# Reordering the side work of a fused RNN, SSM, LSTM and adapter kernel

## The chip, the cores and the metric

The kernel runs on one core of a Trainium2 chip, as one launch. The metric is the device time in microseconds. The engines named below are PE (TensorE: matmuls, with PEld for its weight loads), DVE (VectorE), ACT (ScalarE), POOL (GpSimd) and SP, which here only issues DMAs. Every engine works through its own instruction list in the order in which the kernel wrote it; semaphores make an instruction wait for another engine.

## The reference, cut to what matters

Four layers with residuals, over x of shape (4, 1024, 512), batch B = 4, T = 1024, D = 512. The first and the third are recurrences over the 1024 steps.

```python
x = x + rnn(x)        # h = tanh(x_t @ Wx + b + h @ Wh), h0 = cond
x = x + ssm(x)        # below
x = x + lstm(x)       # A = x_t @ Wx + b + h @ Wh; i, f, o, g; c; h = o * tanh(c)
x = x + adapt(x)      # out = x @ (base + x_a x_b^T), one layer matrix per batch row
...
# ssm: a convolution over 4 steps, two projections, and a state of 64 channels
proj = conv @ Wp + bp;  B_t = softplus(proj[..., :N]);  C_t = tanh(proj[..., N:])
u = x @ Ws + bs
state = decay * state + dt * b_t * u_t;  y_t = c_t * state
out = y @ Wo + bo
# adapt: x_a and x_b come from the condition alone
h = gelu(layernorm(cond) @ w1 + b1);  xw = h @ w2 + b2     # w2: 512 x 8192
```

## The kernel before, in words

All four layers run at once, on different parts of the sequence. Time is cut into 32 chunks of TC = 32 steps. `do_pass(c)` runs the 32 LSTM steps of chunk c; in the same steps the RNN runs LEAD = TC + 20 = 52 steps ahead, and between the two the kernel puts what the chunks between need: projections, the SSM of chunk c + 1, the inputs of the LSTM, and the adapter of chunk c - 1. In the first 52 steps (pass -2 from step 12 on, and pass -1) there is no LSTM; only the RNN and preparation run. I call these the lead.

The order is written out by hand (`manual_schedule`), so the lists in the code are the order on each engine. In one step of `do_pass` they are:

- PE: the LSTM's 96 matmuls (`lstm_mm`, L362; bf16, the state as three bf16 parts), then the jobs placed as "pe", then `rnn_mm` (L337), then whatever the step's "early" jobs issue.
- DVE: for half A of the LSTM state the transpose (L379), sum (L384), products, cell, h (L408) and two splits (L191), then the same for half B. Jobs placed as "gap" come between B's cell and B's h. After B come `rnn_pre` (transpose L345, add L346), then the jobs placed as "end", then "early" jobs.
- ACT: the tanh of gates and cell, two small copies for the next step, the RNN's tanh (L349), and the ACT parts of the jobs.

A job is a triple of step, place and function. Those of a regular pass, before:

- `adapt_jobs`: four adds at the end of steps 1, 2, 5 and 6; the four products `ada` (L702, each 4 matmuls with 512 columns) in steps 16, 21, 22, 23; in the end place of 23 an ACT copy and four output DMAs.
- `ssm_jobs`: three adds x + h in steps 9 to 11; `taps` in 12 to 15 (16 matmuls with 128 columns each) and `skip` (8 matmuls) in 16; the softplus in 15 to 23; four scans, then y = state * dt * c, in place in tile w; then the output product in 24.
- `project0`: the RNN's input projection of chunk c + 3, 16 matmuls with 128 columns in each of steps 17 to 20.
- `input_jobs`: the LSTM's input product for 8 steps at a time, 4 matmuls with 512 columns a step (L318), in steps 0 to 11 and 25 to 28, followed by two transposes (L322) and two bias adds (L330).

fp32 matmuls show as two records each in the profile, bf16 ones as one.

The lead also prepares: the LSTM weights are loaded and split in three bf16 parts (`split_wh2`, ACT L276 and L280, DVE L277 and L281), one piece a step from step 5 to 20. `adapt_hidden` computes the hidden layer at step 30. From step 32 on `adapt_w2(j)` multiplies one piece of w2 (two ranks, 512 KB, four buffers) at a time: 16 matmuls with 64 columns, a copy on ACT, and the load of piece j + 4. Twelve pieces come in the lead, one every step and a half, and twenty in steps 0 to 19 of pass 0. `adapt_gather` brings the results into another layout by DMAs on POOL, `base_identity` adds 2 to a diagonal by 16 small DVE instructions, `adapt_sum` adds the gathered parts, and `adapt_layer` makes the layers, one of 16 tiles a step from step 25 of pass 0.

Of the kernel before, what the change touches and what calls it, by code (L numbers as in the profile page):

```python
# [14 lines left out]
P = 128  # L15
B, T, D = 4, 1024, 512
KC = D // P
# [3 lines left out]
TG = 8  # L21
LEAD = TC + 20
CT = 32
# [15 lines left out]
def cond_resid_kernel(ctx: ExitStack, tc: tile.TileContext, a: dict, out: bass.AP):  # L39
# [293 lines left out]
    def rnn_mm(c, t):  # L333
        h = h0[c % 2] if t else h0[(c - 1) % 2]
        for k in range(KC):
            for j in range(4):
# [4 lines left out]
                )  # L341

    def rnn_pre(c, t):
        tt, pre = tt0[0], pre0[t % 2]
        nc.vector.transpose(tt.rearrange("p c b -> p (c b)"), acc0)  # L345
        nc.vector.tensor_add(pre, xw0[c % 2][:, :, t, :], tt[:, :, :B])  # L346
# [71 lines left out]
    def ssm_jobs(c):  # L418
# [6 lines left out]
        def add(ms, t0, t1):  # L425
            t = lambda y: y[:, ms, t0:t1].rearrange("p c t b -> p c (t b)")
            v.tensor_add(t(x1[:, :, 3:, :]), t(x), t(h))  # L427


        jobs = [  # L430
            (9, "end", lambda: add(slice(0, 2), 0, TC - 4)),
            (10, "gap", lambda: add(slice(2, 4), 0, TC - 4)),
            (11, "end", lambda: add(slice(0, 4), TC - 4, TC)),
        ]
# [17 lines left out]
        cg, z, e, u, w, p = (sm(n) for n in ("cg", "z", "e", "u", "w", "p"))  # L452
        bt, vv, y = z, e, w
        v3, y3 = (t.rearrange("p (t b) -> p t b", b=B) for t in (vv, y))
        y_last = y3[:, TC - 1, :]
        jobs += [(12 + k, "pe", lambda k=k: taps(k)) for k in range(KC)]
        jobs.append((16, "pe", skip))

        def turn(n):
            cols = slice(n * TOK // 4, (n + 1) * TOK // 4)  # L460
            v.reciprocal(u[:, cols], u[:, cols])


        jobs += [
            (15, "end", lambda: act.activation(z, pb[:NS, 0, :], AF.Identity, bias=vec[:NS, 0:1])),
            (15, "end", lambda: act.activation(e, pb[:NS, 0, :], AF.Abs, bias=vec[:NS, 0:1])),
            (16, "end", lambda: act.activation(e, e, AF.Exp, scale=-1.0)),
            (16, "end", lambda: act.activation(u, e, AF.Copy, bias=2.0)),
            (18, "end", lambda: act.activation(cg, pb[NS:, 0, :], AF.Tanh, bias=vec[NS:, 0:1])),
            (18, "end", lambda: v.tensor_mul(u, u, e)),  # L470
            (18, "end", lambda: v.tensor_mul(w, u, u)),
            (18, "end", lambda: act.activation(p, w, AF.Copy, scale=2.0 * SERIES[-1])),
            (23, "end", lambda: act.copy(s1, y_last)),
        ]
# [7 lines left out]
        for b in range(B):  # L482
# [4 lines left out]
        chain += [  # L487
            lambda: v.scalar_tensor_tensor(y, y, dt, cg, ALU.mult, ALU.mult),
        ]
        place = lambda n: ("gap", "end", "end")[n % 3]  # L490
        jobs += [(17 + n // 3, place(n), lambda n=n: turn(n)) for n in range(4)]
        jobs += [(19 + n // 3, place(n), f) for n, f in enumerate(chain)]

# [27 lines left out]

    xr = w1.rearrange("p k (a r n) -> p (k a) r n", a=2, n=P // 2).rearrange(
        "p (h d) r n -> p h d r n", h=2
    )
    raw = [work.tile([P, D], F32, name=f"raw{i}", tag=x) for i, x in enumerate(("x3", "x4"))]
# [52 lines left out]
    def adapt_w2(j):  # L578


        half, hd, rg = j // (KC * RANK // WR), j // (RANK // WR) % KC, j % (RANK // WR)
        ps = bank("pp", [P, P // 2])
        for k in range(KC):
            for t in range(4):
                n0 = P // 2 * (t % 2)
                nc.tensor.matmul(
                    ps[CT * t : CT * (t + 1), :], hid[:, k, :], w2[j][:, t // 2, k, n0 : n0 + P // 2],
                    start=(k == 0), stop=(k == KC - 1),
                )
        nc.scalar.copy(xr[:, half, hd, rg], ps)  # L590
        if j + W2_BUFS < NW2:
            load_w2(j + W2_BUFS)

    def adapt_gather(half):

        for t in range(4):
            for g in range(RANK // WR):
                nc.gpsimd.dma_start(
                    out=raw[half].rearrange("(b r) n -> b r n", r=32)[:, WR * g + t // 2].rearrange(
                        "b (d h n) -> b h d n", d=KC, h=2  # L600
                    )[:, t % 2],
                    in_=xr[CT * t : CT * t + B, half, :, g],
                )
# [59 lines left out]
    at_step(21, load_base)  # L663
    at_step(20, fold_conv)
    for half in range(2):
        at_step(27 + half, lambda half=half: adapt_bias(half))
    at_step(24, adapt_center)
    at_step(25, adapt_norm)
    at_step(26, lambda: nc.scalar.activation(b2[:, 3], b2[:, 3], AF.Copy, scale=2.0))
    for k in range(KC):  # L670
        at_step(26 + k, lambda k=k: double_g(k))
    at_step(30, adapt_hidden)
    NPRE = 12
    for j in range(NW2):
        f = lambda j=j: adapt_w2(j)
        if j < NPRE:
            at_step(32 + 3 * j // 2, f)
        else:
            at(0, j - NPRE, f)
        if j % (NW2 // 2) == NW2 // 2 - 1:  # L680
            at(0, j - NPRE, lambda half=j // (NW2 // 2): adapt_gather(half))
    for half in range(2):
        at(0, 24, lambda half=half: adapt_sum(half))
    at(0, 23, base_identity)
    for n in range(B * KC):
        c, t = divmod(25 + n, TC)
        at(c, t, lambda n=n: adapt_layer(n % B, n // B))


    def adapt_jobs(c, dst):  # L690
# [21 lines left out]

        jobs = [((1, 2, 5, 6)[m], "end", lambda m=m: add(m)) for m in range(KC)]
        jobs += [((16, 21, 22, 23)[k], "pe", lambda k=k: mm(k)) for k in range(KC)]
        return jobs + [(23, "end", end)]


    def input_jobs(c, n, t):
        ps = {}

        def mm(k):
            if not ps:

                ps[0] = bank("proj2", [P, D], tag=("ada", "po")[n % 2], bufs=1)
            input_mm(c, n, k, ps[0])

        last = t + KC - 1
        return [(t + k, "pe", lambda k=k: mm(k)) for k in range(KC)] + [
            (last, "end", lambda: input_turn(c, n, 0, ps[0])),
            (last + 1, "gap", lambda: input_turn(c, n, 2, ps[0])),  # L730
            (last + 1, "end", lambda: input_bias(c, n, 0)),
            (last + 2, "gap", lambda: input_bias(c, n, 2)),
        ]


    def do_pass(c, first=0, src=None, dst=None):
# [5 lines left out]
        if -1 <= c < NCHUNK - 1:  # L742
            jobs += ssm_jobs(c + 1)
            jobs += input_jobs(c + 1, 0, 25)
        if src is not None:
            jobs.append((12, "end", lambda: load_x(c + 4, src)))
        if c + 3 < NCHUNK:
            for m in range(KC):
                mm, end = project0(c + 3, m)
                jobs += [(17 + m, "pe", mm), (17 + m, "end", end)]  # L750
        if lstm:
            for n in range(1, TC // TG):
                jobs += input_jobs(c, n, KC * (n - 1))

# [5 lines left out]
        for t in range(first, TC):  # L760
# [10 lines left out]
            if rnn:  # L771
                rnn_mm(*r)
            if lstm:
                A.transpose()
# [105 lines left out]
```

## Time and profile before

| | us |
|---|---|
| median of 3 runs | 4822.73 (4818.03 to 4823.34) |
| the profiled execution | 4822.13 |
| its span | 4820.3 |
| TensorE busy | 4609.6 |
| DVE busy | 3864.6 |
| ACT busy | 1494.4 |
| LSTM matmuls L362, 98304 records | 2881.0 |
| RNN matmuls L337, 32768 records | 1109.8 |
| input products L318, 4096 records | 528.9 |

Busy time is what an engine's records cover; a matmul's record includes time in which the next one has already begun, so the distance from the start of one group to the start of the next says more. "Idle before, releaser" in a line names what ended an engine's wait. A releaser "issue" means that nothing the profile shows held the engine back. The table by stage has, for each stretch, its length, the busy time of PE, PEld, DVE, ACT and POOL with the number of instructions, the granted TensorE clock (1.00 is full), the share of the DMA engines and GB/s.

The instructions of TensorE are themselves fetched by DMA:

```profile
q8 instruction: 1149, 18.83, 1.6%
```

### The profile page before, as it was taken

The page shows a single profiled execution, that of the slowest core. Times are in us where ns is not written, and L with a number is a line of the kernel's source. Part 1 is how long each engine was busy: PE and PEld are TensorE (multiplying, and loading weights), DVE is VectorE, ACT ScalarE, POOL GpSimd, SP SyncE. Part 2 cuts the span into 40 slices and gives each one's busy share as a digit, 9 for nine tenths or more (in the row PEclk, how much of TensorE's full clock was granted, in tenths as well). Part 3 has the DMA queues.
Part 4 walks back from the last instruction along what each step waited for, and adds up shares of the span by engine and source line. Part 5 has one row for each costly group of instructions (what it writes and reads, how often), then busy time and mean ns, then how long its engine had stood idle before and what let it go on. Part 6 is the DMA issues. An engine that isn't in the chain of part 4 may idle for free.

```text
span 4820.3 us, 320719 instructions
## 1 busy us (share of the span) xinstructions
PE 4609.6 (96%) x147040; PEld 3536.0 (73%) x147040; DVE 3864.6 (80%) x18001; ACT 1494.4 (31%) x7661; POOL 53.5 (1%) x96
## 2 busy tenths in 40 slices
PE   6899999999999999999999999999999999999976
PEld 4777777777777777777777777777777777777754
DVE  3578888888888888888888888888888888888876
ACT  2223333333333333333333333333333333333322
POOL 2000000000000000000000000000000000000000
PEclk7999999999999999999999999999999999999999
DMA  6300000000000000000000000000000000000000
GB/s 146 115 9 9 9 7 9 7 9 9 9 7 9 7 9 9 9 7 9 6 9 9 9 7 9 7 9 9 9 7 9 7 9 9 9 4 6 6 6 7
DMA packets 38780, 67.41 MB, mean 14 GB/s; under 512 B 9056, under 2 KB 26080, under 8 KB 36400
## 3 DMA queue, kind: packets, MB, share of 16 engines
q1 hardware_dynamic: 34064, 46.68, 3.7%
q8 instruction: 1149, 18.83, 1.6%
q14 instruction: 207, 1.70, 0.1%
q0 software_dynamic: 2208, 0.19, 0.1%
q10 hardware_dynamic: 1152, 0.01, 0.0%
HBM read 38.34 MB, written 8.39 MB: 10 GB/s over the span
## 4 chain that ended last, share of the span: by engine, by line
PE 89%; DVE 8%; issue 1%; ACT 1%; DMA 0%; ACTq 0%; SPq 0%; DVEq 0%
PE acc L362 57%; PE acc L337 16%; PE proj L318 9%; PE pb L292 3%; PE proj L292 2%; DVE tt L379 2%; PE ada L702 2%; DVE gc L384 1%; DVE h L191 1%; DVE h L408 1%; DVE prod L395 1%; DVE gc L400 1%; DVE tt L345 0%; ACT x L709 0%; PE pl L624 0%
## 5 line engine op out<-in xcount | busy, mean ns | idle before, releaser
L362 PE MATMUL acc<-wh,h 128*12 128x256 bf16 x98304 | 2881.0, 273 | 145.8 <-DVE h L191 135.6
L362 PEld LDWEIGHTS <-h 128*12 128x12 bf16 x98304 | 2276.8, 88 | 702.6 <-DVE h L191 382.5
L379 DVE STREAM_TRANSPOSE tt<-acc 128x256 f32<-128x256 f32 x2048 | 918.8, 449 | 453.0 <-PE acc L362 334.9
L337 PEld LDWEIGHTS acc<-wh,h 128*4 128x4 f32 x32768 | 816.9, 87 | 505.1 <-issue 206.6
L337 PE MATMUL acc<-wh,h 128*4 128x128 f32 x32768 | 1109.8, 275 | 34.9 <-ACT h L349 25.2
L391 ACT ACTIVATE gc<-gc 128x32 f32<-128x32 f32 x2048 | 469.8, 229 | 1319.0 <-DVE gc L384 1233.0
L384 DVE TENSOR_REDUCE gc<-tt 128x32 f32<-128x128 f32 x2048 | 774.2, 378 | 35.3
L191 DVE TENSOR_TENSOR h<-h 128x8 f32<-128x8 f32 (+1 forms) x4098 | 681.2, 166 | 104.8
L405 ACT ACTIVATE th<-gc 128x8 f32<-128x8 f32 x2048 | 427.8, 209 | 826.2 <-DVE gc L400 826.2
L349 ACT ACTIVATE h<-pre 128x16 f32<-128x16 f32 x1024 | 221.3, 216 | 1149.7 <-DVE pre L346 1149.7
L318 PE MATMUL proj<-wx,x 128*32 128x512 f32 x4096 | 528.9, 592 | 0.6 <-DVE x L500 0.6
L408 DVE SCALAR_TENSOR_TENSOR h<-gc,th 128x8 f32<-128x8 f32 x2048 | 342.4, 167 | 141.3 <-ACT th L405 126.3
L345 DVE STREAM_TRANSPOSE tt<-acc 128x128 f32<-128x128 f32 x1024 | 316.2, 309 | 68.3 <-PE acc L337 65.2
L400 DVE SCALAR_TENSOR_TENSOR gc<-prod 128x8 f32<-128x8 f32 x2048 | 341.9, 167 | 35.5
L368 ACT COPY tt<-xw 128x32 f32<-128x32 f32 x2048 | 327.7, 207 | 0.0
L395 DVE SCALAR_TENSOR_TENSOR prod<-gc 128x16 f32<-128x16 f32 x2048 | 318.1, 155 | 0.0
L346 DVE TENSOR_TENSOR pre<-xw,tt 128x16 f32<-128x16 f32 x1024 | 179.8, 176 | 37.0
L292 PE MATMUL proj<-xin,wx 128*32 128x128 f32 x4096 | 144.9, 277 | 14.1 <-DMA wh<-in_Wh_dram 10.8
L292 PE MATMUL pb<-x,wp 128*32 128x128 f32 x4096 | 136.8, 273 | 3.3 <-DVE x L427 1.8
L702 PE MATMUL ada<-layer,x 128*32 128x512 f32 x1024 | 135.0, 600 | 3.0 <-DVE x L695 3.0
L292 PEld LDWEIGHTS proj<-xin,wx 128*32 128x32 f32 x4096 | 119.8, 112 | 16.5 <-DMA wh<-in_Wh_dram 10.7
L318 PEld LDWEIGHTS proj<-wx,x 128*32 128x32 f32 x4096 | 118.0, 110 | 6.2 <-DVE x L500 0.7
(116 smaller groups left out, 1152.7 us busy)
## 6 DMA issues: line engine op xcount, KB each, us to landing
layer<-in_w2T_dram SPq DMA_DIRECT2D x32, 512.0 KB, 3.5
xin<-in_xT_dram SPq DMA_DIRECT2D x128, 64.0 KB, 2.3
out_dram<-x SPq DMA_DIRECT2D x128, 64.0 KB, 1.7
layer<-in_Wh_dram SPq DMA_DIRECT2D x16, 256.0 KB, 10.0
wx<-in_Wx_dram SPq DMA_DIRECT2D x4, 1024.0 KB, 15.5
wx<-in_Wx_dram SPq DMA_DIRECT2D x4, 256.0 KB, 4.4
wh<-in_Wh_dram SPq DMA_DIRECT2D x4, 256.0 KB, 6.8
layer<-in_w_dram SPq DMA_DIRECT2D x4, 256.0 KB, 23.0
```

What stands on the lines that cost most here:

```text
L191: nc.vector.tensor_tensor(h[:, :, n], h[:, :, n - 1], upper(h[:, :, n - 1]), ALU.subtract)
L292: nc.tensor.matmul(dst[CT * j : CT * (j + 1)], columns(j), x, start=first, stop=final)
L318: nc.tensor.matmul(ps[CT * j : CT * (j + 1), :], tok, w[:, j], start=(k == 0), stop=(k == KC - 1))
L337: nc.tensor.matmul(acc0[CT * j : CT * j + B, :], h[:, k, (t - 1) % TC, :], wh0[:, k, j * P : (j + 1) * P], start=(k == 0), stop=(k == KC - 1),
L362: nc.tensor.matmul(acc2[mh][CT * j : CT * j + NP * B, :], parts, w[:, :, n0 : n0 + 2 * CT], start=(k == 0 and n == 0), stop=(k == KC - 1 a ...
L379: nc.vector.transpose(self.tt[:, :, :, B:].rearrange("p g c b -> p (g c) b"), acc2[self.m])
L384: nc.vector.tensor_reduce(self.gc[:, :4].rearrange("p g c b -> p (g c) b"), self.tt[:, :, :, : (1 + NP) * B].rearrange("p g c (s b) -> p ( ...
L391: nc.scalar.activation(self.gc[:, :4], self.gc[:, :4], AF.Tanh, scale=0.5)
L395: nc.vector.scalar_tensor_tensor(self.prod, self.gc[:, 0:2], 1.0, self.gc[:, 3:5], ALU.add, ALU.mult)
L400: nc.vector.scalar_tensor_tensor(self.c, self.prod[:, 1], 0.5, self.prod[:, 0], ALU.mult, ALU.add)
L405: nc.scalar.activation(self.th, self.c, AF.Tanh, scale=0.5)
L408: nc.vector.scalar_tensor_tensor(self.out[:, :, 0], self.gc[:, 2], 1.0, self.th, ALU.add, ALU.mult)
```

## The change

LEAD becomes TC + 24, so the RNN runs 56 steps ahead and the lead has 56 steps. In a regular pass the jobs move:

| | before | after |
|---|---|---|
| SSM adds | 9 end, 10 gap, 11 end | 5, 6, 7 end |
| `taps` | 12, 13, 14, 15 | 8, 10, 12, 14 |
| `skip` | 16 | 16 |
| `ada` products | 16, 21, 22, 23 | 17, 19, 21, 23 |
| `project0` | 17, 18, 19, 20 | 18, 20, 22, 30 |
| LSTM inputs 1, 2, 3 | 0-3, 4-7, 8-11 | 0-3, 4-7, 9, 11, 13, 15 |
| adapt adds | 1, 2, 5, 6 end | 0, 1, 2 end, 6 gap |
| copy of the last state | 23 end | 24 end |
| x load | 12 | 9 |

The scans write a tile of their own, `states`, and y goes to tile p. `adapt_w2` takes two pieces of w2 at once, with 128 columns a matmul, every third step from step 35 of the lead and every second step of pass 0; the gathers are half as many. `keep_busy` adds four matmuls with 512 columns, whose result nobody reads, behind `rnn_mm` in the first 32 steps. `adapt_layer` runs three times in four steps, from step 24. In the lead, steps of single preparations move by one.

```diff
-LEAD = TC + 20
+LEAD = TC + 24
...
+    idle = bank("idle", [P, D], tag="ada", bufs=1)
+    def keep_busy():
+        x = xin[0].rearrange("p c t b -> p (c t b)")
+        tiled(idle, lambda j: x[:, :CT], x)
...
-            (9, "end", lambda: add(slice(0, 2), 0, TC - 4)),
-            (10, "gap", lambda: add(slice(2, 4), 0, TC - 4)),
-            (11, "end", lambda: add(slice(0, 4), TC - 4, TC)),
+            (5, "end", lambda: add(slice(0, 2), 0, TC - 4)),
+            (6, "end", lambda: add(slice(2, 4), 0, TC - 4)),
+            (7, "end", lambda: add(slice(0, 4), TC - 4, TC)),
...
-        bt, vv, y = z, e, w
-        v3, y3 = (t.rearrange("p (t b) -> p t b", b=B) for t in (vv, y))
+        bt, vv, states, y = z, e, w, p
+        v3, y3 = (t.rearrange("p (t b) -> p t b", b=B) for t in (vv, states))
...
-        jobs += [(12 + k, "pe", lambda k=k: taps(k)) for k in range(KC)]
+        jobs += [(8 + 2 * k, "pe", lambda k=k: taps(k)) for k in range(KC)]
...
-            (23, "end", lambda: act.copy(s1, y_last)),
+            (24, "end", lambda: act.copy(s1, y_last)),
...
-            lambda: v.scalar_tensor_tensor(y, y, dt, cg, ALU.mult, ALU.mult),
+            lambda: v.scalar_tensor_tensor(y, states, dt, cg, ALU.mult, ALU.mult),
...
-        jobs += [(17 + n // 3, place(n), lambda n=n: turn(n)) for n in range(4)]
-        jobs += [(19 + n // 3, place(n), f) for n, f in enumerate(chain)]
+        jobs += [((16, "end"), (16, "end"), (17, "gap"), (17, "end"))[n] + (lambda n=n: turn(n),) for n in range(4)]
+        jobs += [(19 + (n + 1) // 3, place(n + 1), f) for n, f in enumerate(chain)]
...
-        ps = bank("pp", [P, P // 2])
+        ps = bank("pp", [P, P])
         for k in range(KC):
             for t in range(4):
-                n0 = P // 2 * (t % 2)
                 nc.tensor.matmul(
-                    ps[CT * t : CT * (t + 1), :], hid[:, k, :], w2[j][:, t // 2, k, n0 : n0 + P // 2],
+                    ps[CT * t : CT * (t + 1), :], hid[:, k, :], w2[j + t // WR][:, t % WR, k],
...
-        if j + W2_BUFS < NW2:
-            load_w2(j + W2_BUFS)
+        for n in range(j + W2_BUFS, min(j + W2_BUFS + 2, NW2)):
+            load_w2(n)
...
-    for j in range(NW2):
+    for j in range(0, NW2, 2):
         f = lambda j=j: adapt_w2(j)
         if j < NPRE:
-            at_step(32 + 3 * j // 2, f)
+            at_step(35 + 3 * j // 2, f)
         else:
-            at(0, j - NPRE, f)
+            at(0, j - NPRE + 1, f)
...
+    at(0, 21, base_identity)
     for half in range(2):
-        at(0, 24, lambda half=half: adapt_sum(half))
-    at(0, 23, base_identity)
+        at(0, 22 + half, lambda half=half: adapt_sum(half))
     for n in range(B * KC):
-        c, t = divmod(25 + n, TC)
+        c, t = divmod(24 + 4 * n // 3, TC)
...
-        jobs = [((1, 2, 5, 6)[m], "end", lambda m=m: add(m)) for m in range(KC)]
-        jobs += [((16, 21, 22, 23)[k], "pe", lambda k=k: mm(k)) for k in range(KC)]
+        jobs = [((0, 1, 2, 6)[m], ("end", "gap")[m // 3], lambda m=m: add(m)) for m in range(KC)]
+        jobs += [(17 + 2 * k, "pe", lambda k=k: mm(k)) for k in range(KC)]
...
                 mm, end = project0(c + 3, m)
-                jobs += [(17 + m, "pe", mm), (17 + m, "end", end)]
+                t = (18, 20, 22, 30)[m]
+                jobs += [(t, "pe", mm), (t, "end", end)]
...
-                jobs += input_jobs(c, n, KC * (n - 1))
+            jobs += input_jobs(c, 1, range(4), ((3, "end"), (4, "gap"), (4, "end"), (5, "gap")))
+            jobs += input_jobs(c, 2, range(4, 8), ((8, "gap"), (8, "end"), (9, "gap"), (9, "end")))
+            jobs += input_jobs(c, 3, range(9, 17, 2), ((15, "end"), (16, "gap"), (18, "gap"), (19, "gap")))
...
             if rnn:
                 rnn_mm(*r)
+            if c * TC + t < 8 - TC:
+                keep_busy()
```

## The prediction

> **What bounds the kernel now.** I read the totals and the chain of waits first, then the table by stage, then the timeline of single steps.
>
> ```profile
> PE 4609.6 (96%) x147040; PEld 3536.0 (73%) x147040; DVE 3864.6 (80%) x18001; ACT 1494.4 (31%) x7661; POOL 53.5 (1%) x96
> PE 89%; DVE 8%; issue 1%; ACT 1%; DMA 0%; ACTq 0%; SPq 0%; DVEq 0%
> ```
>
> That looks like a TensorE bound. One step of the middle says otherwise:
>
> ```profile
> 1503.64 0.45 DVE L379 STREAM_TRANSPOSE tt<-acc 128x256 f32<-128x256 f32 x1 [0.22 <-PE acc L362]
> 1504.40 1.03 PE L318 MATMUL proj<-wx,x 128*32 128x512 f32 x8
> 1505.26 1.05 PE L337 MATMUL acc<-wh,h 128*4 128x128 f32 x32
> 1506.22 2.80 PE L362 MATMUL acc<-wh,h 128*12 128x256 bf16 x96
> 1508.09 0.45 DVE L379 STREAM_TRANSPOSE tt<-acc 128x256 f32<-128x256 f32 x1 [0.23 <-PE acc L362]
> ```
>
> From transpose to transpose a step takes 4.45 us: a loop of LSTM matmuls, transpose, sum, tanh, products, h, splits and matmuls again. The last steps, which have no other TensorE work, take 4.45 us too, so the loop's latency is the bound. Side work fits in the gaps: 0.86 us of L318 and 0.86 of L337 (start to start) leave TensorE some 0.1 us. DVE has about 0.3 us in the "gap" place and 0.6 at the "end". A step is longer only where a job overflows its gap; those overflows are what a reordering can win.
>
> ```profile
> 0.00:162.15 162.15, 108.60 (x2774) 80.83 (x2777) 62.43 (x214) 44.08 (x131) 35.44 (x64) 0.82 0.58 142
> 162.15:331.31 169.16, 157.93 (x5193) 129.72 (x5184) 126.40 (x580) 47.21 (x256) 18.02 (x32) 0.99 0.18 56
> 331.31:485.50 154.19, 151.35 (x4586) 112.37 (x4578) 124.27 (x568) 45.84 (x237) 0.00 (x0) 1.00 0.03 8
> 485.50:4525.00 4039.50, 3962.84 (x127540) 3048.81 (x127535) 3341.01 (x15652) 1280.57 (x6631) 0.00 (x0) 1.00 0.03 8
> ```
>
> These stages are the lone RNN, pass 0, pass 1 and passes 2 to 29 (then 283 us for the last two passes, 12 for the tail). A pass without overflow is 32 x 4.453 = 142.5 us. Passes 2 to 29 take 4039.5 / 28 = 144.27, so 1.77 each is to be had; pass 0 is 26.7 over, pass 1 11.7.
>
> **The steady passes.** By step number, averaged over passes 3 to 28, the 1.77 lies in four places.
>
> ```profile
> 2432.76 1.03 PE L702 MATMUL ada<-layer,x 128*32 128x512 f32 x8
> 2433.61 0.93 PE L292 MATMUL pb<-x,ws 128*32 128x128 f32 x14
> 2468.09 0.59 ACT L709 COPY x<-ada 128x512 f32<-128x512 f32 x1
> 2468.58 0.19 ACT L473 COPY s<-w 64x4 f32<-64x4 f32 x1
> 2468.80 0.34 DVE L488 SCALAR_TENSOR_TENSOR w<-w,sp,cg 64x128 f32<-64x128 f32 x1 [0.90 <-ACT s L473]
> 1706.28 0.83 PE L362 MATMUL acc<-wh,h 128*12 128x256 bf16 x23 [0.29 <-issue]
> ```
>
> - Step 16, +0.76: one `ada` product and the `skip` matmuls share a step, 0.86 + 0.55 where 0.96 fits. After, `skip` keeps step 16 and `ada` goes to 17, 19, 21, 23, alone in each: 0.
> - Step 23, +0.48: y overwrites the states, so DVE waits 0.90 us for the copy of the last state, which stands behind the 0.59 us output copy on ACT; A's transpose is queued behind it. After, y has its own tile and the copy goes to step 24: 0. Late next is DVE's own work, a scan and y, which ends at 4.45: nothing to wait for.
> - Step 11, +0.09: the last add waits for the same step's RNN h and a 0.44 us turn follows. After, the add is at step 7 with no turn behind it, ending 4.46 into the step: 0 to 0.03.
> - Steps 13 to 20, +0.41 in all, irregular, idle put down to "issue". Instruction queue q8 moved 18.83 MB in 1149 packets: 64 bytes for each of TensorE's 294,080 records, 256 a packet. A step with 64 small records beside the 256 of LSTM and RNN uses 320, one with L318 or `ada` 272. The four tap steps and four projection steps follow each other, and the stalls start only at the second. Steps 0 to 11, at 272, have none. After, 320 and 272 alternate: 296 on average, between the two. Bounds: 0 (as at 272) and 0.41 (as now). The first tap step after the light ones costs 0.01, so I take 0.12.
>
> The moved DVE jobs make step 16 (0.44 in the gap, two reciprocals at the end), 18 and 19 (0.42 and 0.56) the fullest. Today's step 17 has 0.34 and 0.62 and costs nothing by itself. I count them zero, with 0.02 each above. Adapt adds and turns move one at a time to places with as much room; x loads on SP go three steps earlier, past nothing that waits. New pass: 142.65. Gain 28 x (144.27 - 142.65) = **45.4 us**. The last two passes have almost no overflow.
>
> **Pass 0.**
>
> ```profile
> 173.36 1.06 PE L337 MATMUL acc<-wh,h 128*4 128x128 f32 x32
> 174.24 0.63 PE L586 MATMUL pp<-layer,hid 128*32 128x64 f32 x32
> 174.68 2.58 PE L362 MATMUL acc<-wh,h 128*12 128x256 bf16 x87
> 339.41 1.12 PE L624 MATMUL pl<-xt,xt 8*128 8x512 f32 x2
> ```
>
> A w2 piece takes 0.44 us from start to start (32 records of 64 columns) and lengthens a full step by 0.35. A pair has 32 records of 128 columns. Here a rule speaks for more: the Trainium skill (TensorE: Matmul & The Clock Gate, "Wait — 56ns, not 53.3ns?") says that start-to-start never drops below about 25 ns, however small the matmul. By it 64 columns cost as much as 128 and pairs would halve the time. The row shows 14 ns for 64 columns and L337's 27 for 128, so a pair is 0.87 us, two pieces' worth. I take the row; by the rule it would be 3 to 6 us better. Ten pairs fall in steps 1, 3, ... 19; 17 and 19 have no product in pass 0. So 8 x 0.77 = 6.2 us against 20 x 0.35 = 7.
>
> The larger part is stalls: what these steps have beyond 4.80 sums to 10.2 us, nearly all in steps 4 to 18, at 336 and 384 records a step while w2 streams. Pairs halve w2's records, so two steps average 304, later 328; a 272-record step costs 0, the 336 of steps 0 to 9 cost 0.2 a step, so I take 3 (1 to 8). `base_identity` and the sums (4.5 today) remain about 4.1, moved to steps 21 to 23; gathers are issued from step 19, 8 instead of 16 each at 0.57 us on POOL, and land well before 23. Six of the 16 layer products come in this pass, 5.6 against 5.1 for seven: each costs 1.05 in a full step, 0.1 to 0.3 in an empty one. Sum 142.5 + 6.2 + 3 + 4.1 + 5.6 = 161.4: **-7.8**. Pass 1 has ten layer products instead of nine (10.5 against 9.5) and the steady 1.6 and stalls off: **-1.1**.
>
> **The lead**, 52 steps today, 56 then.
>
> ```profile
> 50.00:60.00 10.00, 7.17 (x126) 3.75 (x116) 6.72 (x15) 4.37 (x11) 0.10 (x1) 0.50 1.01 209
> 90.00:95.00 5.00, 5.00 (x66) 3.85 (x70) 1.72 (x9) 2.11 (x4) 0.00 (x0) 0.50 0.01 3
> 55.19 1.89 PE L337 MATMUL acc<-wh,h 128*4 128x128 f32 x32 [0.90 <-ACT h L349]
> ```
>
> The granted clock is 0.50 from 45 us to 100, L337 takes 1.89 us instead of 1.06 and a step 2.78 instead of 1.96 to 2.02. The skill's same page ("Why this matters for your kernels") asks for no idle gap over about 3 us. A 4.65 us fetch gap at 34.5 fits; but afterwards the gaps are 0.9 us, and the clock stayed low for 50 us, until matmuls filled TensorE wholly (5.00 of 5.00). By the rule fillers would buy nearly nothing; by the rows they buy the difference. I take the rows. A filler has L318's shape: 0.86 us, in a wait of 1.08 us between two L337 groups; hidden. At half clock it would not fit.
>
> In steps 5 to 20 DVE and ACT split weights: L280, L276, L281, L277 in turn bound a step at 2.52, so only 0.26 is won there. By intervals between RNN steps: 0 to 3 stay 8.0. 4 to 8: 20.2, with two fetch stalls, become 16 (fillers add 16 records a step, the four projections take 256 out; 12 to 22). 9 to 20: 34.3 become 31.4 (three get a projection's ACT copy, +0.4). 21 to 27: 21.2 become 16.2. 28 to 30: 6.9 become 6.2. 31 to 50: 52.2, which is 12.2 over 20 x 2.0, become 24 intervals at 2.0 plus 9: four places where a w2 pair meets other products (0.6 each), the hidden layer behind a filler (1.6), waits and table loads (5). From the first `pre` at 18.1 to the last: 152.9 against 161.0. **-8** (-18 to +14). w2 loads want 1 MB per three steps, 160 GB/s, under the 209 reached above.
>
> **Sum.** 45.4 + 7.8 + 1.1 + 8 = 62.3 off the profiled execution's own 4822.1 (span 4820.3; median of the runs 4822.7, the same within 0.6): **4760 us**.
>
> **Rivals.**
> 1. Stalls stay with the alternation (0.41 a pass): 28 x 0.29 = 8 less, and 3 less in pass 0: 4771. For it: the fetch total per pass is unchanged.
> 2. The start-up gives back: four steps more (+8), clock gain lost to more fetching, pass 0 unchanged: 4822 - 45 - 1 + 8 = 4784. For it: DMA is full from 20 to 80 us.
> 3. Slower: an isolated 320-record step drains the fetch every time. Nine such steps a pass (taps, projections, `out_mm`) at today's typical stall of 0.45 give 4.05 x 28 = 113 against 54 of other gains: 4881. It decides from 0.21 us a step. Against it: the first tap step and `out_mm`, both 320, stall hardly at all.
> 4. The overflows are replaced by equal ones in the fuller DVE steps, and the start-up is a draw: about 4820.
>
> **Chances.** Forecast 0.60, rivals 0.12, 0.16, 0.07, 0.05. 0.2% (9.6 us) is what a measurement of this kernel can tell from no change: faster 0.88, same 0.05, slower 0.07. The range: lead and stalls at their good ends give 4738; rival 2 with some stalls left gives 4792.
>
> **What would show it.** Right: steps 16 and 23 at 4.45; L488 with no wait on L473; no "issue" idle of note after steps 13 to 20; clock near 1.0 from 50 us; first LSTM transpose near 154. Wrong: any regular step over 4.5, fillers starting at half clock, L337 waiting for a filler.

## The result and the profile after

The changed kernel takes 4770.6 us (median of 4 runs, 4770.0 to 4771.8) against 4823.0 for the kernel before on the same chip (4818.0 to 4825.7): a ratio of 0.989, 95% interval 0.988 to 0.991. The profiled span goes from 4820.3 us to 4768.2. The time came from where the prediction looked for it, with two terms too large. First the totals and the chain of waits of the changed kernel:

```profile
PE 4608.4 (97%) x146784; PEld 3524.3 (74%) x146784; DVE 3867.3 (81%) x18001; ACT 1493.9 (31%) x7645; POOL 45.6 (1%) x80
PE 94%; DVE 4%; DMA 1%; issue 1%; ACT 0%; SPq 0%; ACTq 0%; DVEq 0%
```

TensorE is busy 1.2 us less, and the run is 52 us shorter. The totals hide that the lead, with fillers and four more steps, is busy 16.1 us longer (124.69 against 108.60); in passes 2 to 29 it is busy some 11 us less. So most of the gain is idle time; in the chain, DVE's share has gone from 8% to 4%. Now the table by stage (start and end, length, busy time of PE, PEld, DVE, ACT and POOL, granted clock, DMA share, GB/s):

```profile
0.00:158.16 158.16, 124.69 (x2965) 84.81 (x2969) 63.40 (x222) 44.96 (x129) 36.55 (x64) 0.98 0.59 146
158.16:321.37 163.21, 155.22 (x4870) 122.97 (x4862) 125.63 (x579) 46.78 (x246) 9.05 (x16) 0.99 0.17 58
321.37:474.68 153.31, 151.74 (x4591) 112.26 (x4582) 125.09 (x570) 45.83 (x237) 0.00 (x0) 1.00 0.03 8
474.68:4473.71 3999.03, 3951.84 (x127564) 3044.08 (x127555) 3344.50 (x15653) 1280.64 (x6632) 0.00 (x0) 1.00 0.03 8
```

| stage | before | predicted | after | gain |
|---|---|---|---|---|
| lead, to the first LSTM transpose | 162.15 | 154 | 158.16 | 4.0 |
| pass 0 | 169.16 | 161.4 | 163.21 | 6.0 |
| pass 1 | 154.19 | 153.1 | 153.31 | 0.9 |
| passes 2 to 29 | 4039.5 | 3994.2 | 3999.03 | 40.5 |
| one of these | 144.27 | 142.65 | 142.82 | |

The prediction's last stage of before ends at 4525.00, 0.65 us short of the pass; from first transpose to first transpose the 28 passes took 4040.1 (144.29 each), so their gain is 41.1, and the last passes hold next to nothing of the 52.1. The clock of the lead rose from 0.82 to 0.98, as meant, and the lead is only 4.0 us shorter. That gap is the most instructive part of the case; the other is step 24 of each pass.

**The regular steps.** Two stretches of the timeline of the same pass (start, length, engine, line, operation, out<-in, shapes, count, and in brackets the idle time before it and what ended it): TensorE in step 16, then DVE and ACT in step 23.

```profile
2403.02 0.93 PE L292 MATMUL pb<-x,ws 128*32 128x128 f32 x14
...
2407.48 0.60 PE L703 MATMUL ada<-layer,x 128*32 128x512 f32 x4
```

`skip` (L292 `pb`) is alone now, and `ada` comes only with the next step: step 16 lasts 4.47 instead of 5.21.

```profile
2437.32 0.27 DVE L490 TENSOR_TENSOR_SCAN w<-decay,s,e 64x32 f32<-64x32 f32 x1
2437.62 0.34 DVE L495 SCALAR_TENSOR_TENSOR p<-w,sp,cg 64x128 f32<-64x128 f32 x1
2437.92 0.45 DVE L386 STREAM_TRANSPOSE tt<-acc 128x256 f32<-128x256 f32 x1
```

The scan, y (L495, into tile p) and the transpose follow each other with no wait in brackets. Step 23 lasts 4.46 instead of 5.11. (The prediction's +0.48 was the net of steps 23 and 24 of before: 5.11 + 4.28 against twice 4.455.) The irregular "issue" stalls are 0.1 us a pass; 0.12 was predicted.

**Step 24.** This one I had at no cost, and it takes 4.606, 0.15 too long in every pass. It is the regular step over 4.5 that I had named as a sign of being wrong. TensorE, then its weight loads, in step 24:

```profile
2438.78 1.08 PE L292 MATMUL ssm_out<-p,wo 64*32 64x128 f32 x32
2439.79 1.06 PE L337 MATMUL acc<-wh,h 128*4 128x128 f32 x32
2438.78 0.81 PEld L292 LDWEIGHTS ssm_out<-p,wo 64*32 64x32 f32 x32 [0.22 <-issue]
2439.79 0.77 PEld L337 LDWEIGHTS acc<-wh,h 128*4 128x4 f32 x32 [0.20 <-issue]
```

The output product has 32 records of 128 columns, like L337, and L337's usual distance to the next group is 0.87. Here it is 2439.79 - 2438.78 = 1.01. The weight loads before the product and behind it wait 0.22 and 0.20 us for "issue". The product is the only one of the pass that runs on 64 rows of the array ("64*32"); all others have 128. In the kernel before the same product followed the late step 23, and step 24 was 4.28 long; the cost was hidden in that delay. But the distance of 1.01 stood in that trace too:

```profile
2469.28 1.08 PE L292 MATMUL ssm_out<-w,wo 64*32 64x128 f32 x32
2470.29 1.06 PE L337 MATMUL acc<-wh,h 128*4 128x128 f32 x32
```

**Pass 0.** A pair of w2 pieces (L589) and a stall, on TensorE:

```profile
194.18 1.05 PE L589 MATMUL pp<-layer,hid 128*32 128x128 f32 x32
195.06 2.79 PE L369 MATMUL acc<-wh,h 128*12 128x256 bf16 x96
202.00 1.91 PE L369 MATMUL acc<-wh,h 128*12 128x256 bf16 x61 [1.34 <-issue]
```

The pair takes 195.06 - 194.18 = 0.88 and its step 5.22, so +0.77, just the predicted size; the w2 steps in 1 to 15 take 5.22 to 5.24 but for step 11, and step 17 costs nothing. The stalls do not go entirely: 1.6 in step 8, 0.5 in 11, 1.4 in 12, 0.4 in 16, 1.1 in 23.

**The lead.** Intervals between one RNN step's `pre` and the next, in sums:

| RNN steps | before | predicted | after |
|---|---|---|---|
| up to the first | 18.1 | 18.1 | 19.0 |
| 0 to 3 | 8.0 | 8.0 | 7.95 |
| 4 to 8 | 20.2 | 16 | 15.8 |
| 9 to 20 | 34.3 | 31.4 | 35.9 |
| 21 to 27 | 21.2 | 16.2 | 17.2 |
| 28 to 30 | 6.9 | 6.2 | 6.4 |
| the rest | 52.2 | 57 | 54.7 |

Steps 9 to 20 got longer, although the clock is high. TensorE at 51 us, what the DMA queues moved in that stretch (51 to 54.5 us; packets, MB, share of 16 engines), and a row of the 10 us that follow, by the columns of the stage table:

```profile
51.00 0.82 PE L337 MATMUL acc<-wh,h 128*4 128x128 f32 x20 [0.61 <-ACT h L356]
53.83 0.50 PE L337 MATMUL acc<-wh,h 128*4 128x128 f32 x10 [2.00 <-issue]
...
55.38 2.13 PE L292 MATMUL proj<-xin,wx 128*32 128x128 f32 x30
```

```profile
q1 hardware_dynamic: 105, 0.74, 99.0%
q8 instruction: 1, 0.02, 2.4%
```

```profile
60.00:70.00 10.00, 7.56 (x152) 3.89 (x144) 6.05 (x14) 4.61 (x11) 0.00 (x0) 1.00 1.02 214
```

L337 stops in the middle of a group of 32 and goes on 2.00 us later, with nothing to wait for but its next instructions. Queue q1, which loads weights, has the DMA engines almost to itself, and one packet of instructions arrives in 3.5 us. There are two such gaps, in steps 12 and 15 (intervals of 4.31 and 3.75 instead of 2.5 to 2.8; the second gap is 1.82). Step 13 (4.28) has none: behind the first gap the granted clock is 0.50 from 54.4 to 57.9 us, and a filler and the projection behind it take twice their time (2.13 us instead of 1.06). L337, whose input is ready at 55.26, starts at 57.08 behind them. A filler at half clock does not fit, as the prediction had said, and L337 waiting for one was a sign of being wrong.

That these are waits for instructions, the traces of all runs show together. In the eight kernels with the fillers and the early load of `wx2` (the changed kernel, `e2_inplace`, `e2b_inplace`, `e3_runs`, `e4_single`, `e5_scan`, `e7_share`, `e8_pad`) TensorE's "issue" gaps of over 1 us in steps 4 to 20 stand behind the 349th, 477th, 732nd or 860th matmul record, whatever job that is. These are 128, 255 and 128 apart, and 128 matmuls with their 128 weight loads are the 256 instructions of a packet (one record seems to be missing). Each of these gaps ends 1.3 to 1.9 us after a packet of q8 has landed.

### The profile page after: what moved, and what is told of

It reads as the page before. It is cut to its first block, busy times and chain, and to the rows that moved or that the text cites. A ratio compares the mean times of both kernels' runs of the same rounds, so it can differ in the third digit from the quotient of the medians.

```text
span 4768.2 us, 320158 instructions
## 1 busy us (share of the span) xinstructions
PE 4608.4 (97%) x146784; PEld 3524.3 (74%) x146784; DVE 3867.3 (81%) x18001; ACT 1493.9 (31%) x7645; POOL 45.6 (1%) x80
## 4 chain that ended last, share of the span: by engine, by line
PE 94%; DVE 4%; DMA 1%; issue 1%; ACT 0%; SPq 0%; ACTq 0%; DVEq 0%
PE acc L369 59%; PE acc L337 18%; PE proj L318 9%; PE pb L292 3%; PE proj L292 2%; PE ada L703 2%; DVE tt L386 1%; DVE gc L391 1%; DVE h L191 1%; PE ssm_out L292 1%; DMA layer<-in_w_dram 1%; DVE h L415 0%; DVE prod L402 0%; DVE gc L407 0%; PE pl L625 0%
## 5 line engine op out<-in xcount | busy, mean ns | idle before, releaser
L337 PEld LDWEIGHTS acc<-wh,h 128*4 128x4 f32 x32768 | 805.4, 87 | 510.0 <-issue 214.8
L337 PE MATMUL acc<-wh,h 128*4 128x128 f32 x32768 | 1086.1, 273 | 18.1 <-ACT h L356 11.0
L191 DVE TENSOR_TENSOR h<-h 128x8 f32<-128x8 f32 (+1 forms) x4098 | 680.5, 166 | 104.8
L292 PE MATMUL proj<-xin,wx 128*32 128x128 f32 x4096 | 137.9, 278 | 11.1 <-DMA wx<-in_Wx_dram 11.1
L292 PE MATMUL pb<-x,wp 128*32 128x128 f32 x4096 | 134.4, 273 | 0.0
L292 PEld LDWEIGHTS proj<-xin,wx 128*32 128x32 f32 x4096 | 117.5, 112 | 14.9 <-DMA wh<-in_Wh_dram 11.1
```

Source lines behind the costliest of these rows:

```text
L191: nc.vector.tensor_tensor(h[:, :, n], h[:, :, n - 1], upper(h[:, :, n - 1]), ALU.subtract)
L292: nc.tensor.matmul(dst[CT * j : CT * (j + 1)], columns(j), x, start=first, stop=final)
L337: nc.tensor.matmul(acc0[CT * j : CT * j + B, :], h[:, k, (t - 1) % TC, :], wh0[:, k, j * P : (j + 1) * P], start=(k == 0), stop=(k == KC - 1),
```

## The experiments

Each changes the new kernel, but for `b1_fill`. "Passes 2 to 29" is the mean length of one in the profiled execution; what only passes and steps can show is read from there. Ratios are against the kernel before on the same chip (its medians were 4812 to 4829 us on the four chips), so totals are compared only among kernels of one chip.

| kernel | chip | median us | ratio, interval | passes 2 to 29 |
|---|---|---|---|---|
| e1_nofill | 1 | 4767.2 | 0.9872 [0.9856, 0.9889] | 142.83 |
| e2_inplace | 1 | 4791.1 | 0.9923 [0.9908, 0.9938] | 143.45 |
| e3_runs | 1 | 4779.8 | 0.9899 [0.9885, 0.9914] | 143.15 |
| e7_share | 1 | 4793.2 | 0.9927 [0.9912, 0.9942] | 143.63 |
| e4_single | 2 | 4776.3 | 0.9890 [0.9875, 0.9905] | 142.86 |
| e5_scan | 2 | 4769.4 | 0.9874 [0.9857, 0.9890] | 142.81 |
| e6_fill21 | 2 | 4768.2 | 0.9872 [0.9857, 0.9886] | 142.80 |
| b1_fill | 2 | 4826.3 | 0.9995 [0.9987, 1.0004] | 144.52 |
| e2b_inplace | 3 | 4779.8 | 0.9926 [0.9910, 0.9943] | 143.10 |
| e8_pad | 3 | 4763.3 | 0.9894 [0.9879, 0.9909] | 142.60 |
| e10_late | 3 | 4769.0 | 0.9905 [0.9891, 0.9920] | 142.76 |
| e9_best | 4 | 4756.8 | 0.9887 [0.9870, 0.9903] | 142.57 |

### The regular passes

**e7_share** puts `ada` back beside `skip`.

```diff
-        jobs += [(17 + 2 * k, "pe", lambda k=k: mm(k)) for k in range(KC)]
+        jobs += [((16, 19, 21, 23)[k], "pe", lambda k=k: mm(k)) for k in range(KC)]
```

> The changed kernel with the first adapter product back in step 16 beside skip; step 17 has no product then. Theory (TensorE has room for 0.96 us of products in a step): step 16 goes from 4.47 to about 5.21 us, 0.75 a pass, 21 us over passes 2 to 29, with nothing won in the empty step 17. Rival (the empty step that follows gives it back): under 0.1 a pass.

Measured: step 16 takes 5.225, step 17 returns to 4.45 without giving anything back, and the pass is 0.80 longer. TensorE in that step:

```profile
2413.43 1.03 PE L703 MATMUL ada<-layer,x 128*32 128x512 f32 x8
2414.29 0.93 PE L292 MATMUL pb<-x,ws 128*32 128x128 f32 x14
2415.06 1.03 PE L337 MATMUL acc<-wh,h 128*4 128x128 f32 x28
```

`ada` takes 0.86 from start to start and `skip` another 0.77 before L337 runs on undivided; the gap holds one of them. (The prediction had `skip` at 0.55, and 0.86 + 0.55 - 0.96 is only 0.45; its 0.76 was read from the steps.) This step of the sum stands, and it is worth 28 x 0.77 = 22 us.

**e2_inplace** lets y overwrite the states again, with the copy of the last state in step 23.

```diff
-        bt, vv, states, y = z, e, w, p
+        bt, vv, states, y = z, e, w, w
...
-            (24, "end", lambda: act.copy(s1, y_last)),
+            (23, "end", lambda: act.copy(s1, y_last)),
```

> The changed kernel with y written over the states again and the copy of the last state back in step 23. Theory (DVE waits for a small ACT copy behind the output copy, and A's transpose stands behind DVE): steps 23 and 24 together go from 9.06 us to about 9.39 as before the change, 0.33 a pass, 28 x 0.33 = 9 us over passes 2 to 29. Rival (the wait is only taken over by the output product's own wait for y): no change in the sum of the two steps.

The pass grew by 0.63, twice the expectation. The edit did more than I meant: by the order of the list the copy now stands ahead of the last scan, so the carried state of one batch row is that of a chunk earlier, and the scan waits for the copy as well as y does. It measures two waits at once and decides nothing. **e2b_inplace** is the same with the last scan moved ahead of the copy, as in the kernel before.

```diff
-        jobs += [(19 + (n + 1) // 3, place(n + 1), f) for n, f in enumerate(chain)]
+        jobs += [((22, "end") if n == 11 else (23, "gap") if n == 12 else (19 + (n + 1) // 3, place(n + 1))) + (f,) for n, f in enumerate(chain)]
```

> The kernel with the third scan at the end of step 22 and the fourth in the gap of 23, and with y written over the states and the copy of the last state in step 23, so in the order of the kernel before. Compared with the same kernel with y apart (142.81 us a pass, steps 23 and 24 together 9.07). Theory (DVE waits for the copy behind the output copy): the two steps take 9.39 as before the change, 0.32 a pass, 9 us over passes 2 to 29. Rival (the 0.63 a pass of the first version came from the last scan standing behind the copy, not from y): no more than 0.1 a pass.

DVE in step 23:

```profile
2446.89 0.34 DVE L495 SCALAR_TENSOR_TENSOR w<-w,sp,cg 64x128 f32<-64x128 f32 x1 [0.90 <-ACT s L480]
```

The wait of 0.90 us for the copy behind the output copy is back. Steps 23 and 24 take 5.12 + 4.28 = 9.40 instead of 9.07, and the pass is 0.30 longer than in `e5_scan`, which has its own tile for y and the same placing of the scans. So the separate tile, with the copy in step 24, is worth 0.3 a pass and not 0.48: the rest comes back in step 24, which needs 4.61 once it no longer starts late.

**e5_scan** has only that move of the scans. It asks whether step 24 is long because y ends too late.

> The changed kernel with the third scan at the end of step 22 and the fourth in the gap of 23, so that y ends about 0.2 us earlier. Theory (step 24 lasts 4.61 us because the output product starts 0.10 late, waiting for y, and is itself 0.05 longer than the room): it starts at 0.76 after the transpose, step 24 falls to about 4.51, and passes 2 to 29 gain 2 to 3 us, less if the third scan delays step 23's transpose by up to 0.05. Rival (the product's own length alone): step 24 stays at 4.60.

y now ends 4.19 us into step 23, well ahead of the product, and step 24 still takes 4.607. The wait for y is not the cause.

**e8_pad** runs the output product on all 128 rows: the upper half of y's tile and of `wo` is zero, so the product's value and its number of records are the same.

```diff
+    wo = const.tile([P, D], F32, name="wo", tag="wo")
+    nc.gpsimd.memset(wo[NS:], 0.0)
...
+    yfull = small.tile([P, TOK], F32, name="yfull", tag="p", bufs=1)
+    nc.gpsimd.memset(yfull, 0.0)
...
-                tiled(po[0][:, m, :], lambda j: wo[:, P * j + CT * m : P * j + CT * (m + 1)], y)
+                tiled(po[0][:, m, :], lambda j: wo[:, P * j + CT * m : P * j + CT * (m + 1)], yfull)
```

> The changed kernel with the output product of step 24 on 128 rows instead of 64: the lower rows hold y, the upper ones zeros, in y and in the weights. The same 32 records. Theory (the 0.15 us of step 24 is the change from 128-row to 64-row matmuls and back, some 0.1 us each, which the trace shows as 0.20 instead of 0.10 between groups of four): the product takes 0.87 us from start to start instead of 1.01, starts at 0.76, and step 24 falls from 4.605 to 4.46; passes 2 to 29 gain 4 us. Rival (the wait for y, or DVE): 4.60 stays.

TensorE in step 24:

```profile
2436.78 1.05 PE L296 MATMUL ssm_out<-yfull,wo 128*32 128x128 f32 x32
2437.65 1.14 PE L341 MATMUL acc<-wh,h 128*4 128x128 f32 x32
```

From start to start 2437.65 - 2436.78 = 0.87 instead of 1.01, step 24 takes 4.46, and a pass 142.60. On the same chip `e10_late`, whose passes are the changed kernel's, has 142.76 a pass, and 4764.7 to 4772.5 in total against 4762.7 to 4764.5. So changing from 128 rows to 64 and back is what the 0.15 us pays for. The traces agree: inside the product of 64 rows the records come in fours every 0.11 us, as in L337, and only before it and behind it are the distances 0.20 instead of the usual 0.10, which the padding brings back. In this run hardly a step of passes 3 to 28 was irregular any more (none by over 0.14); but `e10_late` had few as well (142.76 with a floor of 142.73), so I don't put that down to the padding.

**e3_runs** puts the taps in 8 to 11, the LSTM inputs 3 in 12 to 15, `project0` in 18, 19, 20 and 30 and `ada` in 17, 21, 22, 23: the same work, no alternation.

```diff
-        jobs += [(8 + 2 * k, "pe", lambda k=k: taps(k)) for k in range(KC)]
+        jobs += [(8 + k, "pe", lambda k=k: taps(k)) for k in range(KC)]
...
-        jobs += [(17 + 2 * k, "pe", lambda k=k: mm(k)) for k in range(KC)]
+        jobs += [((17, 21, 22, 23)[k], "pe", lambda k=k: mm(k)) for k in range(KC)]
...
-                t = (18, 20, 22, 30)[m]
+                t = (18, 19, 20, 30)[m]
...
-            jobs += input_jobs(c, 3, range(9, 17, 2), ((15, "end"), (16, "gap"), (18, "gap"), (19, "gap")))
+            jobs += input_jobs(c, 3, range(12, 16), ((15, "end"), (16, "gap"), (18, "gap"), (19, "gap")))
```

> The changed kernel with the tap steps 8 to 11 and the projection steps 18 to 20 in a row again, and the 512-column products in a row behind them. Theory (320-record steps in a row run ahead of the instruction fetch): 0.3 us more a pass, about 8 us over passes 2 to 29, as irregular steps of 4.6 to 5.4 us after the second tap step. Rival (the stalls depend on the records of a whole pass, or are chance): the same 142.8 us a pass.

The pass grows by 0.33, nearly all of it irregular. A piece of a group of 96 that broke off and went on, on TensorE, in a step 20 of 5.35 us:

```profile
1287.61 1.58 PE L369 MATMUL acc<-wh,h 128*12 128x256 bf16 x49 [0.18 <-issue]
```

On average the stalls sit in steps 9 to 12 (0.14 in step 11) and 19 to 21 (0.11 in step 20), that is in the later steps of a run and behind it, up to 0.9 in one step. With 320 and 272 records in turn they are nearly gone. The sum per pass is the same, so here the order of the dense steps counts and not their number. These stalls are waits for instructions as well: in passes 2 to 29, all 13 "issue" gaps of over 0.1 us of TensorE in this run and all 14 in the kernel before end 1.34 to 1.60 us after a packet of q8 has landed, though the packets land some 4 us apart.

### Pass 0

**e4_single** goes back to single w2 pieces and their gathers.

```diff
-        ps = bank("pp", [P, P])
+        ps = bank("pp", [P, P // 2])
...
-                    ps[CT * t : CT * (t + 1), :], hid[:, k, :], w2[j + t // WR][:, t % WR, k],
+                    ps[CT * t : CT * (t + 1), :], hid[:, k, :], w2[j][:, t // 2, k, n0 : n0 + P // 2],
...
-    for j in range(0, NW2, 2):
+    for j in range(NW2):
```

> The changed kernel with w2 taken piece by piece again, 64 columns a matmul, from the lead's step 35 and in steps 0 to 19 of pass 0, with the old gathers. Theory (a pair costs TensorE what two pieces cost; what pairs save is instruction records): steps with a piece and no stall last 4.80 us, two of them 0.1 less over the floor than one step with a pair (0.77), but stalls come back, and pass 0 takes 5 to 8 us more than 163.2. Rival (a pair costs what one piece costs, by a floor on the time of a small matmul): pass 0 takes more by 10 x 0.35 even where no step stalls. Passes 2 to 29 stay.

Pass 0 takes 167.7; the kernels with pairs scatter over 160.8 to 166.0, the two on the same chip have 161.9 and 165.0. TensorE in a step with a single piece:

```profile
162.96 0.63 PE L593 MATMUL pp<-layer,hid 128*32 128x64 f32 x32
163.40 2.80 PE L369 MATMUL acc<-wh,h 128*12 128x256 bf16 x96
```

A piece takes 0.44 us and an unstalled step 4.80, so two cost 0.70 against 0.77 for a pair. The work is no cheaper in pairs, as the row said; by the floor of some 25 ns a matmul (the Trainium skill, TensorE: Matmul & The Clock Gate, "Wait — 56ns, not 53.3ns?") two single pieces would have cost about twice a pair. But that floor does not describe these groups of four on 32 columns of the array each, whose records start some 7 ns apart, and the next four 36 ns (64 columns) or 90 ns (128) later. What pairs save is stalls: beyond the unstalled lengths, steps 0 to 20 of pass 0 sum to 10.5 us here and to 3.3 to 8.5 in the kernels with pairs.

### The lead

**e1_nofill** leaves out the fillers.

```diff
-            if c * TC + t < 8 - TC:
-                keep_busy()
```

> The changed kernel without the fillers in the first 32 steps. Theory (the fillers keep the clock up and are hidden): the clock falls to 0.50 after a fetch gap and stays there to about 100 us, RNN steps 21 to 27 go from 17.2 us to 20 or more, and the first LSTM transpose comes 3 to 10 us later than the changed kernel's 158.2. Rival (the fillers' own records cause the new fetch gaps of steps 12 to 15, 4.8 us): steps 9 to 20 get shorter by about that and the first LSTM transpose comes no later, or earlier. Passes 2 to 29 stay at 142.8 us each by both.

The first LSTM transpose comes at 158.03 instead of 158.16. The fillers win nothing that shows here. A row of this kernel's lead, in the columns of the stage table:

```profile
60.00:70.00 10.00, 6.64 (x116) 3.76 (x120) 6.17 (x15) 5.01 (x12) 0.00 (x0) 0.50 1.03 218
```

Without fillers the clock is 0.50 here, 1.00 with them, and 0.85 against 0.98 in the mean of the lead, so they do what I said of the clock. It did not stay down, as I had expected, but was 0.50 in four stretches (29.7 to 43.4, 57.0 to 77.5, 80.9 to 91.2 and 101.4 to 104.8 us). Yet the lead is as fast: 4 to 8 take 12.9 us (15.8 with fillers), 9 to 20 take 35.2 (35.9), 21 to 27 take 19.0 (17.2), and step 31, with the hidden layer, 5.85 (4.19). A slow TensorE asks for fewer instructions, and in steps 4 to 20 only short gaps are left, the longest interval being 3.46 in step 14. What the fillers win where DMA is idle they lose where it is full: steps 4 to 20 take 48.1 and 48.3 us in the two changed kernels without fillers there (this one and `e6_fill21`) and 50.3 to 54.4 in the eight with them. The one profile of the kernel before, without fillers too, has 54.5. That the 6 us come from the projections' new places is an inference: no run moves them alone.

**e6_fill21** keeps fillers only in RNN steps 21 to 31, where the load of DMA has ended.

```diff
-            if c * TC + t < 8 - TC:
+            if 21 - LEAD <= c * TC + t < 8 - TC:
```

> The changed kernel with fillers only in the RNN's steps 21 to 31, after the weights' splitting. If the fillers' records cause the fetch gaps of steps 12 to 15 and the clock needs help only afterwards: steps 9 to 20 fall from 35.9 us to 31 to 33 and the first LSTM transpose comes 3 to 5 us earlier than 158.2. If the clock falls at the first gap and stays at 0.50 until step 21: steps 9 to 20 take about 34, as before the change, and the gain is under 2 us or none.

First transpose 158.11, and steps 9 to 20 take 34.3: the second case of the expectation. Steps 21 to 27 take 19.2, so nothing is won there: in this run the clock stays at 1.00 only from about 80 us on. **b1_fill** adds fillers to the kernel before, in its first 32 steps, and nothing else.

> The kernel before with the fillers alone, in its first 32 steps. Theory (the fillers win the clock but their records are fetched while DMA is full): the clock stays near 1.0, steps 21 to 27 fall from 21.2 us to 16 to 18, steps 4 to 20 change by no more than 4 us either way, and the first LSTM transpose comes at 155 to 160 instead of 162.2. Rival (the clock was never the bound of these steps): 162 or later. Passes 2 to 29 stay at 144.3.

First transpose 158.6 instead of 162.15; the whole 4826.3 against 4829.0, with an interval that holds no change. Steps 21 to 27 win 4.3 us, 9 to 20 win 2.0 and 4 to 8 lose 1.2. Pass 0 then takes 2.1 more, so what the lead of this one profile wins, the total doesn't confirm.

**e10_late** tests the gaps: the load of `wx2` (4 MB on SP, at the start) is issued in four parts in steps 22 to 25, and its doubling moves to step 36.

```diff
-    wx2 = load_rows(const, "wx2", a["Wx2"], 4 * D, nc.sync)
+    wx2 = const.tile([P, KC, 4 * D], F32, name="wx2", tag="wx2")
...
+    for j in range(4):
+        at_step(22 + j, lambda j=j: load_wx2(j))
...
-        at_step(27 + k, lambda k=k: double_g(k))
+        at_step(36 + k, lambda k=k: double_g(k))
```

> The changed kernel with the 4 MB load of the LSTM's input weights issued in four parts in the RNN's steps 22 to 25 instead of at the start, and their doubling in steps 36 to 39. Theory (the fetch gaps of the lead come from full DMA): with 4 MB less in front, DMA is no longer full from 45 to 75 us, steps 9 to 20 fall from 35 to 38 us to 31 to 33, and the first LSTM transpose comes at 150 to 156 instead of 156 to 160; if the gaps only move to steps 22 to 31, where DMA is then full, it stays in 156 to 160. Rival (the gaps depend on the number of records alone): no change in steps 9 to 20.

A row and TensorE's gap of this kernel:

```profile
60.00:70.00 10.00, 7.59 (x160) 3.90 (x160) 6.78 (x16) 4.95 (x13) 0.00 (x0) 1.00 0.30 107
98.37 1.24 PE L342 MATMUL acc<-wh,h 128*4 128x128 f32 x19 [2.43 <-issue]
```

With a DMA share of 0.28 to 0.30 from 50 to 70 us, steps 9 to 20 take 31.2 us, which is the 31.4 of the prediction. The gap now stands at 98 us, in the stretch to which the load was moved, and steps 28 to 30 take 10.5 instead of 6.4. So the gaps go with the load of the DMA engines, and putting it elsewhere in one piece moves them: first transpose 159.8.

### A version from the findings

**e9_best** combines the padded output product, `wx2` in single MB at steps 22, 25, 28 and 31 (doubling from step 44), and `base_identity` in quarters at steps 33 to 36, in place of one block of 16 small DVE instructions in step 21 of pass 0.

```diff
+    for j in range(4):
+        at_step(22 + 3 * j, lambda j=j: load_wx2(j))
...
-    at(0, 21, base_identity)
+    for k in range(KC):
+        at_step(33 + k, lambda k=k: base_identity(k))
```

> Three things that the earlier runs point to, together on the changed kernel: the output product on 128 rows, the diagonal of the base added in quarters in the RNN's steps 33 to 36 instead of at once in step 21 of pass 0, and the 4 MB load of the LSTM's input weights in single megabytes in steps 22, 25, 28 and 31. Theory: 142.6 us a pass over passes 2 to 29 (6 us less than the changed kernel), step 21 of pass 0 at 4.5 us instead of 7.5 (3 us less), and with DMA full only for some 5 us at a time fetch gaps of the lead after step 9 under 1.5 us each, so the first LSTM transpose at 152 to 157; in all 4755 to 4762. Rival (each megabyte makes its own gap, as the four together did): 158 to 162 for the first transpose, 4760 to 4766 in all.

4756.8 us (4755.6 to 4758.5). Against the changed kernel's profile: passes 2 to 29 take 3992.1 instead of 3999.0, pass 0 159.6 instead of 163.2 (step 21 falls from 7.51 to 4.45), and the lead 156.8 instead of 158.2, which lies within the scatter of that lead (below). Steps 9 to 20 take 31.2 again; behind them one gap is left, in step 29 (an interval of 4.27), longer than expected, and those of steps 4 to 8 stay (16.5). Its ratio to the kernel before and the changed kernel's overlap, and the two did not run on one chip, so that the total is lower is read from the stages alone.

## Why the prediction was right, and where its sum was off

The mechanism held: a step is as long as the LSTM's loop unless a job overflows its gap, and most of the gain is the overflows of steps 16 and 23 and the stalls of 13 to 20 (with step 11, 41 of 52 us). 62.3 us were forecast and 52.1 came; two terms hold most of the 10. That 4770.6 is also the number of rival 1 (4771) is chance: rival 1 had the stalls of the passes stay, and these went.

- **"16 to 0"** held (4.47; `e7_share` puts the 0.77 back).
- **"23 to 0, nothing to wait for"** held for step 23 and failed in what I let follow it. Step 24 stood in the sum at nothing, as if `out_mm` took a 128-row group's 0.87; it takes 1.01, and the late step 23 had covered the difference. It costs 28 x 0.15 = 4.2 us. The trace of before had the evidence: the 1.01 itself, and a step 24 of 4.28 that was short by 0.17 only because 23 was 0.65 late. What is left of the net 0.48 is 0.48 - 0.15 = 0.33, which `e2b_inplace` measures. `e5_scan` excludes the wait for y, `e8_pad` shows the change of rows.
- **Stalls of 0.12 a pass**: about 0.1. Rival 1 (0.41 stays) and rival 3 (each isolated step of 320 stalls) fall; `e3_runs` shows that the alternation does it.
- **w2 pairs at 0.77**: exact; taking the row and not the skill's floor was right, since the floor does not describe matmuls that run side by side in fours. The stalls of pass 0 were 5 us, not 3, within my bounds of 1 to 8.
- **Lead, "9 to 20 become 31.4"**: 35.9, the second large term, 4.5 us. The time without gaps was right, as `e10_late` shows. I had counted the fillers' 16 records a step for steps 4 to 8 and not for 9 to 20, where the DMA is nearly as full (0.82 to 1.02 from 40 to 70 us). Of the three projections that the change moves into steps 10, 12 and 14 I had counted the ACT copy and not the 64 records each. `b1_fill`, with the fillers and the projections still in steps 5 to 8, takes 21.4 in steps 4 to 8 and 32.3 in 9 to 20, together 53.7, no less than the kernels with the change (50.3 to 54.4): the gaps moved with the records. Rival 2 named this (clock gain lost to more fetching), and in steps 4 to 20 it is what happened. Taking the rows for the clock was right, and the rule of no idle gap over about 3 us (the same page of the skill, "Why this matters for your kernels") does not suffice here: in `e1_nofill` the clock falls at 29.7 us with no gap of TensorE over 0.97 us since it rose at 16.1, in the changed kernel at 54.4 behind the gap of 2.00. Nor did the 4.65 us gap of before hold it down for 50 us, as I had read it: the clock was back at 1.00 from 42.9 to 46.3 and fell again with gaps of at most 1.9. But the high clock bought nothing in sum, since in steps 4 to 20 fetching set the pace. An error the other way hides part of this: the rest of the lead was 2.3 us shorter than I had it.

The size of the lead's gain is itself uncertain: the seven kernels with the changed kernel's lead or nearly that reached the first transpose between 156.1 and 161.3 us, by where the gaps fell. Their mean is about 159, so some 3 us is won against the one profile of before.

Left open: what exactly sets how many instruction packets get through when the DMA engines are full, and why totals of the kernel before differ by 17 us among chips.

## What to carry to other kernels

Where a latency loop sets the step, add up each step's side work against its gap, and price a job that was late before by what it needs on time: a delay removed uncovers what it hid. Count instruction records per unit of time as a resource of their own; spread dense steps among light ones, and keep bulk loads away from stretches that issue many small matmuls. Raising the clock pays only where TensorE's speed, and not its supply of instructions, sets the pace.

## What the runs showed of the hardware

- A group of matmuls on 64 rows between groups on 128 takes 1.01 us from start to start, the same number on 128 rows, with the other half zero, 0.87; the extra is at the two changes (0.20 instead of 0.10 us between groups of four).
- TensorE stood idle for 2.00 us in mid-group while loads took 99% of the DMA engines; the gap moved with the load (2.43 us at 98 us). In eight kernels such gaps stood 128 matmul records or a multiple of that apart, a packet of 256 instructions with the weight loads, and ended 1.3 to 1.9 us after a packet had landed.
- 64-column matmuls in groups of four took 0.44 us per 32 records, 14 ns each, half of the 27 ns of 128 columns.
- The granted clock was 0.50 in 10 us of RNN steps that kept TensorE 66% busy in the record (6.64 of 10 us), and 1.00 with 76% (7.56). That gives no threshold: in `e1_nofill` it was 1.00 from 43.4 to 57.0 us with 54% (7.40 of 13.6).
